# A query product placed between two runs of tiled matmuls in an attention kernel

## The chip, the cores and the metric

The kernel runs on one core of a Trainium2 chip. The metric is the device time of one execution in microseconds (us). Three executions before the change took 798.29, 793.81 and 796.25 us; their median is 796.25 us. A further execution was taken with the hardware profiler: it took 796.67 us, of which the span from the first to the last instruction is 794.9 us. Every time below that belongs to a stage comes from that one execution, counted from the start of the span.

The engines are named as in the profile: PE is TensorE with its matmuls, PEld its weight loads, DVE is VectorE, ACT is ScalarE, POOL is GpSimd, SP is SyncE, which here issues the DMAs.

## The reference

A cross-attention layer with a residual, then a feed-forward layer with low-rank experts and a residual, on 16 batches of 64 tokens of width 512, all in float32. There are 32 heads of width 128. Cut to what matters:

```python
q = (layernorm(x) @ Wq).reshape(b, 64, 32, 128)
k = (ctx @ Wk).reshape(b, 64, 32, 128)
v = (ctx @ Wv).reshape(b, 64, 32, 128)
score = einsum('bqhd,bkhd->bhqk', q, k) / sqrt(128) + position_bias
probs = softmax(where(mask, score, -inf))
x = x + einsum('bhqk,bkhd->bqhd', probs, v).reshape(b, 64, 4096) @ Wo
x = x + base(layernorm(x)) + lora(layernorm(x))   # 8 experts of rank 16
```

## The kernel before

All 1024 tokens are held as 8 tiles of 128. Keys and values of all heads are computed first (lines 312 to 354) and stored to DRAM. Then a loop runs over 16 pairs of heads, numbered p = 0 to 15 (line 504), and the feed-forward layer follows.

Large products are computed to nearly full float32 accuracy from two parts per operand, "high" and "low", in the type float32r: three matmuls stand for one (`mm3`, line 219). Each has a 128x128 weight and 512 moving columns. The projections to keys, values and queries use a Winograd scheme: seven products, in the order 1, 2, 6, 5, 7, 4, 3, in place of eight. For the queries of one pair of heads, each of the seven products is one step of `Queries` (line 454), of six matmuls with 512 columns. A step is called **Q** here. Product 1 fills a PSUM bank, which ACT copies to `u` (line 472); products 6, 7 and 4 go on adding to that bank.

Inside the loop, PE does these jobs for a pair:

- **V** (`pv_mm`, line 429): probabilities of the pair before times its values. The array is cut into four tiles of 64x64. In the trace, each float32 matmul is two weight loads and two matmuls, so that V is 128 weight loads and 128 matmuls of 64 columns.
- **S** (`scores`, line 398): queries times keys, in two tiles of 128x64: 64 weight loads and 64 matmuls of 64 columns. DVE then adds the bias, ACT takes 16 exponentials, and DVE normalises.
- **Q**, seven steps: the queries of the next pair.
- **O** (`proj_o`, line 445), eight steps of six matmuls with 512 columns: the output projection of the pair before.
- **T** (`transpose_p`, line 420), two steps of four transposes: the probabilities of this pair.

The order on PE is the program's own: the whole loop stands under a manual schedule for the tensor engine (line 314). In a pair with p from 1 to 14 it is V, S, and then the string of line 514. The other engines' instructions, SP's DMAs among them, are put in order by a scheduler that sees what each needs. A pair also loads four value blocks (`load_v`, line 375), four key blocks (`load_k`, line 368), two bias blocks (`bias_of`, line 392, with an addition of the mask on POOL), two blocks of the output weight (`load_o`, line 382) and two of query weights (`load_pair`, line 359). The raw query weights of pair p + 2 are loaded, summed on POOL and split by ACT and DVE during pair p.

PSUM has two small banks for S and T, and six banks that Q, O and V take in turn.

Of the kernel before, what the change touches and what calls it, by code (L numbers as in the profile page):

```python
# [23 lines left out]
S = 64  # L24
# [21 lines left out]
def xattn_ffn_kernel(ctx: ExitStack, tc: tile.TileContext, x, ctxT, wq, wk, wv, wo, fside, mask,  # L46
# [17 lines left out]
    def blk(tag, name, dt=F32, shape=(P, 512)):  # L64
        return pools[tag].tile(list(shape), dt, tag=tag, name=name)
# [39 lines left out]
    with ExitStack() as actx:  # L105
# [6 lines left out]
        def small_bank(name):  # L112
            return pss.tile([P, 512], F32, tag="s", name=name)
# [200 lines left out]
        with tc.manual_schedule(engines={nc.tensor.engine}):  # L314
# [44 lines left out]
            def load_pair(p):  # L359
                rq = [blk("raw", "rq", F32, (P, 2, 2, P)) for _ in range(2)]  # L360
                for i in range(2):
                    nc.sync.dma_start(out=rq[i], in_=wq[p, i])
                return rq
# [4 lines left out]
            def load_k(h):  # L368
                kT = []
                for j in range(2):  # L370
                    kT.append(blk("raw", "kT"))
                    nc.sync.dma_start(out=kT[j], in_=kd[h][:, j * HALF:(j + 1) * HALF])
                return kT

            def load_v(p):
                v = []
                for w in range(4):
                    v.append(blk("v", "v", F32, (P, 2, 256)))
                    nc.sync.dma_start(out=v[w], in_=vd[p][:, 2 * w:2 * w + 2, :])
                return v  # L380

            def load_o(p):
                w = []
                for i in range(2):
                    s = blk("raw", "so")
                    nc.sync.dma_start(out=s, in_=wo[p, i])
                    hl = [blk("g", f"w{c}", F32R) for c in "hl"]
                    split(hl[0], hl[1], s)
                    w.append(hl)
                return w  # L390

            def bias_of(h):
                bm = blk("bm", "bm", F32, (P, NT, S))
                nc.sync.dma_start(out=bm, in_=fside[h])
                nc.gpsimd.tensor_tensor(bm, bm, maskb, ALU.add)  # L395
                return bm

            def scores(qT, kT, bm):
                ps = small_bank("pss").rearrange("p (t s) -> p t s", t=NT)
                for t in range(NT):  # L400
                    for a in range(2):
                        n = 4 * (t // 2) + 2 * a + t % 2
                        c = slice((n % 8) * S, (n % 8 + 1) * S)
                        nc.tensor.matmul(ps[a * S:(a + 1) * S, t, :], lhsT=qT[n // 8][:, c],  # L404
                                         rhs=kT[n // 8][:, c], start=True, stop=True)
                p = blk("sn", "p", F32, (P, NT, S))
                nc.vector.scalar_tensor_tensor(p, ps, scale, bm, ALU.mult, ALU.add)
                nm = sm.tile([P, NT], F32, tag="nm", name="nm")
                nc.vector.tensor_reduce(nm, p, AX.X, ALU.max, negate=True)  # L409
                sme = sm.tile([P, NT], F32, tag="sme", name="sme")  # L410
                for t in range(NT):
                    nc.scalar.activation(p[:, t, :], p[:, t, :], AF.Exp, bias=nm[:, t:t + 1],  # L412
                                         accum_out=sme[:, t:t + 1])
                rc = sm.tile([P, NT], F32, tag="rc", name="rc")
                nc.vector.reciprocal(rc, sme)
                nc.vector.tensor_tensor(rc, rc, valid, ALU.mult)
                nc.vector.tensor_tensor(p, p, rc.unsqueeze(2).to_broadcast([P, NT, S]), ALU.mult)  # L417
                return p

            def transpose_p(p):  # L420
                ps = small_bank("pst")
                for g in range(4):
                    nc.tensor.transpose(ps[:, g * P:(g + 1) * P],  # L423
                                        p[:, 2 * g:2 * g + 2, :].rearrange("p t k -> p (t k)"), ident)
                pt = blk("sn", "pt", F32, (P, NT, S))
                nc.scalar.copy(pt, ps.rearrange("p (u q) -> p u q", q=S))
                return pt

            def pv_mm(i, pt, v):
                ps = [bank() for _ in range(2)]  # L430
                for u in range(NT):
                    for b in range(2):
                        r = slice(b * S, (b + 1) * S)
                        for d in range(0, P, S):
                            c = slice(i * P + d, i * P + d + S)
                            nc.tensor.matmul(ps[b][d:d + S, u * S:(u + 1) * S], lhsT=v[u // 2][r, u % 2, c],  # L436
                                             rhs=pt[r, u, :], start=True, stop=True)
                res = []
                for b in range(2):
                    hl = [blk("o", f"o{c}", F32R) for c in "hl"]  # L440
                    split(hl[0], hl[1], ps[b])
                    res.append(hl)
                return res

            def proj_o(t, cts, w):
                ps = bank()
                b, g = divmod(t, 4)
                c = slice(g * P, (g + 1) * P)
                for i, ct in enumerate(cts):
                    mm3(ps, [a[:, c] for a in ct[b]], w[i], i == 0, i == 1)  # L450
                with tc.high_priority(offset=SOON):
                    nc.vector.tensor_tensor(acc[:, t, :], acc[:, t, :], ps, ALU.add)  # L452
# [36 lines left out]
            qs = Queries(load_pair(0), ORDER_Q)  # L489
# [4 lines left out]
            for n, i in enumerate(winograd(mm_tokens(tc_, gv), 2, emit_v(NQ - 1), order=ORDER_Q)):  # L494
                if n == 3:
                    ks = [load_k(0), load_k(1)]
                    bms = [bias_of(0), bias_of(1)]
# [6 lines left out]
            for p in range(NP):  # L504
                last = p + 1 == NP
                if pts is not None:
                    prev = ([pv_mm(i, pts[i], v) for i in range(2)], w)
                ps = [scores(qs.head(i), ks[i], bms[i]) for i in range(2)]
                v = load_v(p)
                if not last:  # L510
                    ks = [load_k(2 * p + 2 + i) for i in range(2)]
                    bms = [bias_of(2 * p + 2 + i) for i in range(2)]
                after = None
                steps = "OOOOOOTOTO" if last else "QQQOOQOQOOQOQOTOT" if p else "QQQQQTQQT"
                pts, t, n = [], 0, 0
                for c in steps:
                    if c == "Q":
                        nxt(1)
                        n += 1
                        if n == 3:  # L520
                            w = load_o(p)
                        if n == 7 and p + 2 < NP:
                            after = Queries(load_pair(p + 2), ORDER)
                        if n == 7 and p + 2 == NP:
                            sar = [blk("raw", "sar", F32, (P, 2, NB)) for _ in range(2)]
                            sbw = [blk("raw", "sbw") for _ in range(KC)]
                            for i in range(2):
                                nc.gpsimd.memset(sar[i][:, :, NAR:NB], 0.0)
                                nc.sync.dma_start(out=sar[i][:, :, 0:NAR], in_=arT[:, 2 * i:2 * i + 2])
                            for kc in range(KC):  # L530
                                nc.sync.dma_start(out=sbw[kc], in_=base_wT[:, kc])
                    elif c == "T":
                        pts.append(transpose_p(ps[len(pts)]))
                    else:
                        proj_o(t, *prev)
                        t += 1
                        if last and t == 2:
                            w = load_o(p)
                qs, nxt = nxt, after
# [168 lines left out]
```

## Time and profile before

| what | value |
|---|---|
| median of three runs | 796.25 us (793.81 to 798.29) |
| the profiled execution: time, span | 796.67 us, 794.9 us |
| granted TensorE clock | 1.00 |
| PE, PEld busy | 775.9 us (98%), 674.7 us (85%) |
| DVE, ACT, POOL busy | 580.0 us (73%), 412.3 us (52%), 143.3 us (18%) |
| DMA queue q1 (data) | 119.42 MB, 45.4% of 16 engines |
| DMA queues q8 and q14 (instructions) | 54 packets, 0.88 MB; 32 packets, 0.26 MB |
| loop over the pairs | from 336.4 us (first S) to 734.1 us (last V) |
| one pair, from V to the next V | 25.58 us in most, up to 27.35 us |
| PE instructions | 6944 weight loads, 6944 matmuls |

A busy share is the union of an engine's instruction times over the span. The ends of matmuls are modelled, so a share near 100% says that PE always had something in flight, and not that it ran at its peak; the step from one start to the next is the better measure of a matmul's cost.

### The profile page before, as it was taken

The page shows a single profiled execution, that of the slowest core. Times are in us where ns is not written, and L with a number is a line of the kernel's source. Part 1 is how long each engine was busy: PE and PEld are TensorE (multiplying, and loading weights), DVE is VectorE, ACT ScalarE, POOL GpSimd, SP SyncE. Part 2 cuts the span into 40 slices and gives each one's busy share as a digit, 9 for nine tenths or more (in the row PEclk, how much of TensorE's full clock was granted, in tenths as well). Part 3 has the DMA queues.
Part 4 walks back from the last instruction along what each step waited for, and adds up shares of the span by engine and source line. Part 5 has one row for each costly group of instructions (what it writes and reads, how often), then busy time and mean ns, then how long its engine had stood idle before and what let it go on. Part 6 is the DMA issues. An engine that isn't in the chain of part 4 may idle for free.

```text
span 794.9 us, 17975 instructions
## 1 busy us (share of the span) xinstructions
PE 775.9 (98%) x6944; PEld 674.7 (85%) x6944; DVE 580.0 (73%) x1056; ACT 412.3 (52%) x1154; POOL 143.3 (18%) x146
## 2 busy tenths in 40 slices
PE   7999999999999999999999999999999999999997
PEld 6989899999999999878888888888888887888786
DVE  6997656565557545687778787788778786878986
ACT  6655444444444445565564556555654555456342
POOL 1021000000006012033211322023211321110352
PEclk9999999999999999999999999999999999999999
DMA  7665545455555443474553454434452455241011
GB/s 262 220 238 199 178 162 179 162 183 174 171 171 175 160 159 133 153 230 149 177 170 89 137 173 161 127 112 161 160 181 79 141 178 168 77 154 54 1 41 66
DMA packets 66374, 120.56 MB, mean 152 GB/s; under 512 B 7536, under 2 KB 8176, under 8 KB 66288
## 3 DMA queue, kind: packets, MB, share of 16 engines
q1 hardware_dynamic: 66288, 119.42, 45.4%
q8 instruction: 54, 0.88, 0.5%
q14 instruction: 32, 0.26, 0.1%
HBM read 83.74 MB, written 35.65 MB: 150 GB/s over the span
## 4 chain that ended last, share of the span: by engine, by line
PE 87%; DVE 7%; ACT 2%; issue 1%; DMA 1%; POOL 0%; ACTq 0%; DVEq 0%; POOLq 0%
PE ps L222 76%; PE pss L404 4%; PE ps L436 4%; PE pst L423 2%; ACT p L412 1%; PE yzv L222 1%; DVE pr L605 1%; DVE x2l L69 1%; DVE o L636 1%; DVE gl L69 1%; DVE nb L94 0%; PE pst L100 0%; DMA raw<-in_wk 0%; DMA vd<-c 0%; ACT lg L594 0%
## 5 line engine op out<-in xcount | busy, mean ns | idle before, releaser
L68 ACT CAST gh<-s 128x512 fp32r<-128x512 f32 (+1 forms) x128 | 65.6, 514 | 144.1 <-PE ps L222 134.0
L69 DVE TENSOR_TENSOR gl<-s,gh 128x512 fp32r<-128x512 f32 (+1 forms) x128 | 72.7, 568 | 44.5 <-ACT gh L68 44.3
L222 PE MATMUL ps<-wh,oh 128*128 128x512 f32 x256 | 101.3, 396 | 0.0
L222 PE MATMUL ps<-wl,oh 128*128 128x512 f32 x256 | 99.8, 390 | 0.0
L222 PE MATMUL ps<-wh,ol 128*128 128x512 f32 x256 | 99.7, 390 | 0.0
L452 DVE TENSOR_TENSOR acc<-acc,ps 128x512 f32<-128x512 f32 x128 | 85.3, 675 | 16.5 <-PE ps L222 15.7
L412 ACT ACTIVATE p<-p,nm 128x64 f32<-128x64 f32 x256 | 85.6, 340 | 6.2 <-DVE nm L409 6.2
L157 POOL TENSOR_TENSOR s<-rq 128x256 f32<-128x256 f32 x32 | 25.1, 784 | 293.4 <-DMA rq<-in_wq 206.0
L395 POOL TENSOR_TENSOR bm<-bm,maskb 128x512 f32<-128x512 f32 x32 | 47.1, 1494 | 74.1 <-DVE maskb L342 40.4
L69 DVE TENSOR_TENSOR gl<-raw,gh 128x512 fp32r<-128x512 f32 x48 | 34.6, 723 | 31.9 <-ACT gh L68 31.9
L222 PEld LDWEIGHTS ps<-wl,oh 128*128 128x128 f32 x256 | 48.0, 188 | 10.1
L222 PEld LDWEIGHTS ps<-wh,ol 128*128 128x128 f32 x256 | 48.1, 188 | 9.8 <-DVE ol L69 0.5
L222 PEld LDWEIGHTS ps<-wh,oh 128*128 128x128 f32 x256 | 48.1, 188 | 9.5
L68 ACT CAST gh<-raw 128x512 fp32r<-128x512 f32 x48 | 29.7, 621 | 48.2 <-PE ps L222 36.5
L69 DVE TENSOR_TENSOR ol<-ps,oh 128x512 fp32r<-128x512 f32 x64 | 39.8, 683 | 15.6 <-ACT oh L68 15.6
L412 ACT ACTIVATION_READ_ACCUMULATOR p<-p,nm 128x1 f32 x256 | 49.1, 192 | 0.0
L479 DVE TENSOR_TENSOR q<-u,ps 128x512 f32<-128x512 f32 x48 | 32.7, 681 | 12.6 <-PE ps L222 12.3
L417 DVE TENSOR_TENSOR p<-p,rc 128x512 f32<-128x512 f32 x32 | 39.5, 1234 | 1.1
L68 ACT CAST wh<-so 128x512 fp32r<-128x512 f32 x32 | 19.7, 616 | 37.7 <-PE ps L222 37.1
L404 PE MATMUL pss<-kT,q 128*64 128x64 f32 x1024 | 34.9, 224 | 4.5 <-issue 4.5
L68 ACT CAST oh<-ps 128x512 fp32r<-128x512 f32 x64 | 33.1, 591 | 7.7 <-PE ps L436 7.7
L404 PEld LDWEIGHTS pss<-kT,q 128*64 128x64 f32 x1024 | 31.9, 138 | 5.9 <-issue 4.5
(226 smaller groups left out, 2246.7 us busy)
## 6 DMA issues: line engine op xcount, KB each, us to landing
kd<-c SPq DMA_DIRECT2D x64, 256.0 KB, 2.9
vd<-c SPq DMA_DIRECT2D x64, 256.0 KB, 2.7
v<-vd SPq DMA_DIRECT2D x64, 256.0 KB, 4.6
kT<-kd SPq DMA_DIRECT2D x64, 256.0 KB, 5.3
raw<-in_wk SPq DMA_DIRECT2D x32, 256.0 KB, 3.2
raw<-in_wv SPq DMA_DIRECT2D x32, 256.0 KB, 3.2
bm<-in_fside SPq DMA_DIRECT2D x32, 256.0 KB, 6.0
rq<-in_wq SPq DMA_DIRECT2D x32, 256.0 KB, 5.2
```

What stands on the lines that cost most here:

```text
L68: nc.scalar.copy(hi, src)
L69: (lo_eng or nc.vector).tensor_tensor(lo, src, hi.bitcast(F32), ALU.subtract)
L157: self.eng.tensor_tensor(r, a, b, op)
L222: nc.tensor.matmul(o, lhsT=a, rhs=b, start=first and n == 0, stop=last and n == 2, skip_group_check=True)
L395: nc.gpsimd.tensor_tensor(bm, bm, maskb, ALU.add)
L404: nc.tensor.matmul(ps[a * S:(a + 1) * S, t, :], lhsT=qT[n // 8][:, c], rhs=kT[n // 8][:, c], start=True, stop=True)
L412: nc.scalar.activation(p[:, t, :], p[:, t, :], AF.Exp, bias=nm[:, t:t + 1], accum_out=sme[:, t:t + 1])
L417: nc.vector.tensor_tensor(p, p, rc.unsqueeze(2).to_broadcast([P, NT, S]), ALU.mult)
L423: nc.tensor.transpose(ps[:, g * P:(g + 1) * P], p[:, 2 * g:2 * g + 2, :].rearrange("p t k -> p (t k)"), ident)
L436: nc.tensor.matmul(ps[b][d:d + S, u * S:(u + 1) * S], lhsT=v[u // 2][r, u % 2, c], rhs=pt[r, u, :], start=True, stop=True)
L452: nc.vector.tensor_tensor(acc[:, t, :], acc[:, t, :], ps, ALU.add)
L479: nc.vector.tensor_tensor(self.blocks[key], s[u], b[bk], ALU.add)
```

## The change

In pairs 1 to 14 the first Q step of the pair is put between V and S; the remaining steps keep their places. In pair 0 and in the last pair S still comes first. Nothing is computed more or less. As the score code moves into the loop over the step string, the loads of the values now stand ahead of the scores in the program, and the loads of keys and bias stand directly behind the scores.

```diff
-                ps = [scores(qs.head(i), ks[i], bms[i]) for i in range(2)]
                 v = load_v(p)
-                if not last:
-                    ks = [load_k(2 * p + 2 + i) for i in range(2)]
-                    bms = [bias_of(2 * p + 2 + i) for i in range(2)]
                 after = None
-                steps = "OOOOOOTOTO" if last else "QQQOOQOQOOQOQOTOT" if p else "QQQQQTQQT"
+                steps = "SOOOOOOTOTO" if last else "QSQQOOQOQOOQOQOTOT" if p else "SQQQQQTQQT"
                 pts, t, n = [], 0, 0
                 for c in steps:
-                    if c == "Q":
+                    if c == "S":
+                        ps = [scores(qs.head(i), ks[i], bms[i]) for i in range(2)]
+                        if not last:
+                            ks = [load_k(2 * p + 2 + i) for i in range(2)]
+                            bms = [bias_of(2 * p + 2 + i) for i in range(2)]
+                    elif c == "Q":
                         nxt(1)
                         n += 1
```

In the built program PE's order differs only in that place, 14 times. On SP, the order of a pair's loads becomes: four value blocks, two of query weights, bias, keys, bias, keys, keys, keys; before, it was three value blocks, two of query weights, the fourth value block, two of bias, four of keys. On ACT, the second copy to `u` (product 6) stands behind eight exponentials rather than six. On DVE, the first split of an output weight block stands ahead of the two score additions rather than behind them, and the first two additions of O to the accumulator stand behind the normalisation of the first head rather than around it.

## The prediction

> **What bounds the kernel.** I read the shares and the chain of waits first, then the waits of PE, then the starts of PE's instructions in single pairs. From the page, the shares, the instruction queue and the chain:
>
> ```profile
> PE 775.9 (98%) x6944; PEld 674.7 (85%) x6944; DVE 580.0 (73%) x1056; ACT 412.3 (52%) x1154; POOL 143.3 (18%) x146
> ...
> q8 instruction: 54, 0.88, 0.5%
> ...
> PE 87%; DVE 7%; ACT 2%; issue 1%; DMA 1%; POOL 0%; ACTq 0%; DVEq 0%; POOLq 0%
> ```
>
> PE carries 87% of the chain, so a microsecond on PE in the loop is one at the end. What PE waits for, from the view of waits (total, times, longest):
>
> ```profile
> PE ps L222 <- ACT t1h L68: 5.3, 1, 5.3
> PE pss L404 <- issue: 4.5, 6, 1.4
> PE ps L635 <- DVE hl L69: 1.2, 3, 0.9
> ```
>
> The first is at the start, the third in the feed-forward layer. The second is all that the loop loses, it is in S alone, and "issue" says that no semaphore was waited for. The timeline of PE in pair 2 and in pair 3 (start, length, operation, count):
>
> ```profile
> 376.70 0.60 PE L423 MATMUL pst<-ident,p 128*128 128x128 f32 x4
> 377.23 2.10 PE L436 MATMUL ps<-pt,v 64*64 64x64 f32 x128
> 379.25 1.03 PE L404 MATMUL pss<-kT,q 128*64 128x64 f32 x28
> 381.33 1.28 PE L404 MATMUL pss<-kT,q 128*64 128x64 f32 x36 [1.05 <-issue]
> 382.54 0.50 PE L222 MATMUL ps<-t1h,gh 128*128 128x512 f32 x1
> ```
>
> ```profile
> 403.57 0.60 PE L423 MATMUL pst<-ident,p 128*128 128x128 f32 x4
> 404.10 2.10 PE L436 MATMUL ps<-pt,v 64*64 64x64 f32 x128
> 406.13 2.09 PE L404 MATMUL pss<-kT,q 128*64 128x64 f32 x64
> 408.14 0.50 PE L222 MATMUL ps<-t1h,gh 128*128 128x512 f32 x1
> 408.48 0.40 PE L222 MATMUL ps<-t1h,gl 128*128 128x512 f32 x1
> 408.71 0.40 PE L222 MATMUL ps<-t1l,gh 128*128 128x512 f32 x1
> ```
>
> In pair 3, S takes 408.14 - 406.13 = 2.01 us; in pair 2 it breaks off after 28 matmuls and takes 382.54 - 379.25 = 3.29 us. Measured like this, S is longer by 0.78, 1.28, 0.77, 0.83, 0.58 and 1.77 us in pairs 1, 2, 5, 9, 12 and 13, and never in the other eight of the fourteen that change: **6.01 us in all**.
>
> **What the stalls are.** Counting PE's instructions in the trace from its first, weight loads and semaphore waits included, the six that come late have the numbers 4801, 5313, 7105, 9409, 11201 and 11713: each is 193 above a multiple of 256. Queue q8 moves 54 packets of 16 KB, one for each 258 of PE's 13,954 instructions. So PE's program comes in blocks of 256 instructions, and PE stood at the edge of a block not yet there. The packets' records agree: one starts at 352.92, 378.92, 457.08, 559.93, 637.63 and 664.12 us, and PE goes on 2.62, 2.41, 2.40, 2.39, 2.60 and 2.41 us later. In the six cases these packets start 0.8 to 1.6 us after PE has begun a block. V is 256 instructions in 2.03 us and S is 128 in 2.01 us, while six Q matmuls are 12 in 1.36 us; only V with S behind it can use up 256 instructions in less time than a refill takes. It happens where a block begins some 30 to 130 instructions into V, as the next then begins in S. That holds for the six pairs and for pair 6, where the block came just in time (packet at 481.74, used at 484.15 us, no gap).
>
> Here a rule speaks against the change's worth. The Trainium skill, page "Runtime: NRT & Kernel Launch", section "Instruction fetch mechanics", says that instructions come in 16 KiB blocks of 256, that PE holds 2048 of them and that crossing a block is mostly hidden. The block size agrees with the trace; the hiding does not, at six edges of 54. By the rule nothing is to be saved and only the cost below remains; by the rows up to 6.01 us are. I take the rows.
>
> **What the change removes.** The same instructions stand before V, and the number of instructions of a pair stays, so blocks begin at the same places of V. The edge in S is now reached later: six Q matmuls add 1.59 us (below), and as they are 12 instructions the edge lies 12 of S's 128 sooner, 0.19 us; the refill gains 1.40 us. Five of the six stalls are shorter and go to nothing; pair 13 keeps 1.77 - 1.40 = 0.37 us. **Saved: 6.01 - 0.37 = 5.64 us.** If packets start as late or later in other executions, up to the 6.01 us are there to lose or to win; the lower end is nothing.
>
> **What it adds.** PE's array is 64x64 tiles in V, 128x64 in S, whole in Q, O and T. Before, a pair has three switches (T to V, V to S, S to Q); after, four (T to V, V to Q, Q to S, S to Q). The Trainium skill, page "TensorEngine Tiling (Array Packing)", section "Tiling Modes", says that a change of tiling mode drains TensorE; it has no price. The trace does, in pair 3: from the last start of one kind to the first of the next it is 0.148 us for V to S, 0.151 for S to Q and 0.202 for T to V, where the step within the kind is 0.058, 0.058 and 0.108: about 0.093 us is added at each, whatever the kinds. Then the first weights load in the open: the first Q matmul takes 0.335 us to the next start in place of 0.227, and some steps after it 0.2345.
>
> A switch from Q to S is not in the trace. Lower end: it drains behind other work, and only the 0.108 us of the first Q matmul are paid again: 14 x 0.108 = 1.5 us. Upper end: S waits for the modelled end of the last Q matmul (0.39 us after its start) and 0.093 us more: 0.26 + 0.108 + 0.03 = 0.40 a pair, 5.6 us. Nearest is T to V, which also goes from the whole array to tiles: the step plus 0.093. So the moved Q takes 0.335 + 4 x 0.2345 + 0.227 + 0.093 = 1.59 us where six steps of 0.227 are 1.36: 0.23 us a pair. V to Q replaces V to S at the same 0.15, and the Q step behind S pays what the first paid before. **Added: 14 x 0.234 = 3.3 us.**
>
> **What moves beside it.**
> - S starts 1.59 us later, so its key buffers come free later and key loads are issued later, by as much. Keys of the next pair landed by 423.4 us in pair 3 and are used at 431.7: hidden.
> - SP's queue is in order. The query-weight loads still wait for S's first half and now for the first split of an output weight, which comes earlier since Q does; the bias loads wait for the score additions, about 1.5 us later. POOL ends its bias additions at 419.6 us in pair 3; they are needed at 433.
> - The first Q needs the bank of the seventh O, whose addition on DVE ended at 428.2 us before a V at 429.7: free. Product 6 adds to the bank that ACT copies after product 1; with S between, this copy has 2 us more.
> - The copy of product 6 waits behind eight exponentials. By an estimate from the rows of pair 3 (S half done at 408.7, 0.7 us each for the score addition and the maximum) the exponentials start near 410.3 us, as before (410.6), because the cast and the copy ahead of them come before S's end; product 7, which needs the copy, starts at 417.8. The normalised second head is ready at 420.1 us and transposed at 429.2. Cost: nothing; if the cover went, 7 us would have to go first.
>
> **Sum** against the profiled execution (796.67 us: span 794.9 and 1.8 around it): -5.64 + 3.28 = -2.4 us, 794.3 us. That execution lies 0.4 us above the median of the three, so from 796.25 I forecast **793.9 us**.
>
> **The rivals.**
> - **Larger gain.** The drain after Q hides (1.5 us) and all 6.01 us go: -4.5, 791.7 us. For it: pair 13's rest depends on one packet that started 1.6 us after its block began, which another execution need not repeat. Against it: every switch in the trace pays 0.09 us.
> - **The toll stands alone, slower.** Executions without the profiler have no refill stalls, or new ones replace them; PE pays the fourth switch: 796.25 + 3.3 = 799.5 us, at the upper toll 801.9. It decides as soon as the stalls saved are below 3.3 us. For it: that I see refills only in the profiled execution, and the rule above. Against it: that execution is as long as the others.
> - **A new wait.** The later S makes its pair's chain (score additions, exponentials, transposes) end too late, or the changed order on SP delays a load for Q: 1 us a pair would be +14 us and 808 us with the rest. Against it: the margins above, 7 us and more.
> - **It does nothing it says.** Excluded: the built order has the six matmuls between V and S 14 times.
>
> **Numbers.** 0.5% is 4 us and about what a measurement can tell from no change: faster means below 792.3, slower above 800.2. Forecast 0.50, almost all of it "within"; larger gain 0.30, of which 0.25 past the line; toll alone 0.14, of which 0.06 past it; a new wait 0.06, nearly all past it. With 0.05 of the forecast's own spread on the fast side: faster 0.30, same 0.59, slower 0.11. The forecast's own range is 792 to 796; to leave out 2 in 10 it has to reach into the larger gain and the toll: 790.3 to 798.6.
>
> **What would show it.** S at 2.01 us in pairs 1, 2, 5, 9 and 12 and at most 0.4 us more in 13; the wait of PE for "issue" in S below 1 us; moved Q to S 0.32 us from last start to first; undisturbed pairs 0.23 us longer than 25.58. I am wrong if S still breaks off in most of the six, if undisturbed pairs grow by over 0.4 us, or if PE waits for DVE, ACT or a DMA in the loop.

## The result, and the profile after

Over 20 executions each, the median went from 797.64 us to **794.34 us** (793.03 to 796.92). The ratio on record is 0.997, 95% interval 0.996 to 0.9979, or 2.4 us (1.7 to 3.2). It is an estimate of its own and not the quotient of these two medians, which differ by 3.3 us; against 44 other executions of the kernel before (median 796.8 us) the difference is 2.5 us. The gain is real and small, between 2 and 3 us.

From the page of the kernel after: the shares, the instruction queue and the chain.

```profile
PE 778.5 (98%) x6944; PEld 673.7 (85%) x6944; DVE 589.1 (74%) x1056; ACT 413.0 (52%) x1154; POOL 144.0 (18%) x146
...
q8 instruction: 54, 0.88, 0.5%
...
PE 88%; DVE 7%; ACT 2%; DMA 2%; issue 1%; POOL 0%; SPq 0%; ACTq 0%; DVEq 0%; POOLq 0%
```

PE is busy for 2.6 us *more* than before, and the kernel is faster. A share of busy time can't tell a stall that went from a drain that came: the ends of the last matmuls before a switch are counted as busy. The number of refill packets is the same; what changed is whether PE waits for them. The waits of PE (total, times, longest):

```profile
PE ps L222 <- ACT t1h L68: 5.4, 2, 4.7
PE ps L636 <- DVE hl L69: 1.2, 3, 0.9
PE ps L222 <- ACT u L193: 1.1, 1, 1.1
PE ps L222 <- DVE q L479: 0.8, 1, 0.8
```

The row "pss L404 <- issue: 4.5, 6, 1.4" of before has no counterpart. Pair 2, which had lost 1.28 us in S, in the timeline of PE (start, length, operation, count):

```profile
378.51 2.10 PE L436 MATMUL ps<-pt,v 64*64 64x64 f32 x128
380.54 0.50 PE L222 MATMUL ps<-t1h,gh 128*128 128x512 f32 x1
380.87 0.40 PE L222 MATMUL ps<-t1h,gl 128*128 128x512 f32 x1
381.11 0.40 PE L222 MATMUL ps<-t1l,gh 128*128 128x512 f32 x1
381.34 0.40 PE L222 MATMUL ps<-t1h,gh 128*128 128x512 f32 x1
381.57 0.39 PE L222 MATMUL ps<-t1h,gl 128*128 128x512 f32 x1
381.80 0.40 PE L222 MATMUL ps<-t1l,gh 128*128 128x512 f32 x1
382.13 2.08 PE L404 MATMUL pss<-kT,q 128*64 128x64 f32 x64
384.14 0.50 PE L222 MATMUL ps<-t2h,gh 128*128 128x512 f32 x1
```

Six query matmuls stand between 380.54 and 382.13, and S then runs through its 64 matmuls in 384.14 - 382.13 = 2.01 us. The refill packet of this edge starts at 380.12 us, and the instruction at the edge (number 5313, the same as before) runs at 382.76. Before, the packet started at 378.92 and PE arrived first. Both packets start about equally long after PE has begun a block (1.19 us after, 1.27 before); what changed is how soon the next edge comes. The moved step has given the packet its time.

Of the fourteen pairs that changed, only pair 13 still breaks off in S:

```profile
665.75 0.40 PE L222 MATMUL ps<-t1l,gh 128*128 128x512 f32 x1
666.07 2.32 PE L404 MATMUL pss<-kT,q 128*64 128x64 f32 x64
668.32 0.50 PE L222 MATMUL ps<-t2h,gh 128*128 128x512 f32 x1
```

Here S takes 668.32 - 666.07 = 2.25 us, some 0.23 over. All stalls in S together are 0.24 us, where they were 6.01. And every pair pays: one without a stall lasts 25.81 us from V to V, where it was 25.58.

| part of the profiled execution | before | after |
|---|---|---|
| time | 796.67 us | 795.94 us |
| first S of pair 0 starts at | 336.44 us | 338.00 us |
| pair 0, first S to V of pair 1 | 14.43 us | 14.68 us |
| pairs 1 to 14, from V to V | 364.24 us | 361.63 us |
| stalls in S | 6.01 us | 0.24 us |
| undisturbed pair | 25.58 us | 25.81 us |

The two profiled executions differ by only 0.7 us. The pairs gained 2.6 us, pair 0 lost 0.25 (its wait for DVE's q, line 479, was 0.60 us and is 0.84), and this execution had lost 1.6 us ahead of the loop, where nothing was edited and PE, POOL and SP do the same work in the same order. Over the eight profiled executions of this study, the first S starts anywhere from 335.19 to 338.00 us, and the difference is there within the first 85 us. The three latest (337.50 to 338.00) belong to the three kernels that have the moved step in pair 1; with one execution each, that may be chance. The timed differences follow the loops: a loss of 1.6 us in every execution would leave 0.7 us of gain, and the interval begins at 1.7. So below, stages of single executions are compared only inside the loop, from the start of the first S of pair 0 to the start of the last V ("the loop": 395.59 us before, 393.28 after), and whole times only as medians.

### The profile page after: what moved, and what is told of

The parts are those of the page before. It is cut to its first block, busy times and chain, and to the rows that moved or that the text cites. A ratio compares the mean times of both kernels' runs of the same rounds, so it can differ in the third digit from the quotient of the medians.

```text
span 794.2 us, 18002 instructions
## 1 busy us (share of the span) xinstructions
PE 778.5 (98%) x6944; PEld 673.7 (85%) x6944; DVE 589.1 (74%) x1056; ACT 413.0 (52%) x1154; POOL 144.0 (18%) x146
## 4 chain that ended last, share of the span: by engine, by line
PE 88%; DVE 7%; ACT 2%; DMA 2%; issue 1%; POOL 0%; SPq 0%; ACTq 0%; DVEq 0%; POOLq 0%
PE ps L222 77%; PE pss L404 4%; PE ps L436 4%; PE pst L423 2%; PE yzv L222 1%; ACT p L412 1%; DMA cT<-in_ctxT 1%; DVE o L637 1%; DVE pr L606 1%; DVE x2l L69 1%; DVE nb L94 1%; DVE gl L69 0%; PE pst L100 0%; DVE we L608 0%; DMA so<-in_wo 0%
## 5 line engine op out<-in xcount | busy, mean ns | idle before, releaser
L395 POOL TENSOR_TENSOR bm<-bm,maskb 128x512 f32<-128x512 f32 x32 | 50.0, 1582 | 73.1 <-DVE maskb L342 40.8
L69 DVE TENSOR_TENSOR gl<-rq,gh 128x256 fp32r<-128x256 f32 x48 | 32.9, 687 | 11.4 <-ACT gh L68 11.4
L479 DVE TENSOR_TENSOR q<-u,ps 128x512 f32<-128x512 f32 x48 | 32.6, 680 | 10.6 <-PE ps L222 10.6
L92 POOL TENSOR_TENSOR rs<-rs,nhalf 128x1 f32<-128x1 f32 x16 | 9.5, 595 | 152.1 <-DVE rs L91 109.2
L404 PEld LDWEIGHTS pss<-kT,q 128*64 128x64 f32 x1024 | 31.2, 138 | 5.6 <-PE ps L222 5.0
L436 PEld LDWEIGHTS ps<-pt,v 64*64 64x64 f32 x2048 | 31.4, 135 | 3.3 <-ACT gh L68 2.2
```

The source lines that it names most:

```text
L69: (lo_eng or nc.vector).tensor_tensor(lo, src, hi.bitcast(F32), ALU.subtract)
L92: nc.gpsimd.tensor_tensor(rs, rs, nhalf[:, 0:n], ALU.pow)
L479: nc.vector.tensor_tensor(self.blocks[key], s[u], b[bk], ALU.add)
```

## The experiments

The theory says that two independent terms make the result: stalls at the edges of PE's instruction blocks, which depend only on where an edge falls, and a toll of 0.23 us for each pair with the fourth switch, which is paid everywhere. The main rival says that the order does it: V and S back to back wait for something of their own, or Q in front is better by itself. Four kernels ran beside 44 executions of the kernel before (median 796.8 us), two more beside 9 (796.77 us). Each ratio is to these and, as above, is not exactly the quotient of the medians.

### Query product first in the six stalled pairs only

```diff
-steps = ... else "QSQQOOQOQOOQOQOTOT" if p else "SQQQQQTQQT"
+steps = ... else "QSQQOOQOQOOQOQOTOT" if p in (1, 2, 5, 9, 12, 13) else "SQQQOOQOQOOQOQOTOT" if p else "SQQQQQTQQT"
```

> The query step stands between V and S only in pairs 1, 2, 5, 9, 12 and 13, those whose S broke off before the change; the other eight have V directly before S. My theory (S breaks off where a block of PE's instructions is not yet there, at places fixed by the count of instructions): S takes 2.0 us in all fourteen pairs, at most 0.3 us more in 13; six pairs grow by 0.23 us. Saved 5.8, paid 1.4: 4.4 us below the kernel before, ratio 0.9945. Rival 1 (the stall is a property of V directly before S, and only turned up in these six by chance): about as much stall as before turns up in the eight unprotected pairs, ratio 0.998 to 1.002. Rival 2 (the gain of the change is made by the new order on ACT, DVE and SP, in every pair alike): 6/14 of the 3.3 us measured, ratio 0.998.

Measured, over 11 executions: 793.73 us, ratio 0.996 (0.9947 to 0.9973). The stalls in S are 0.10 us (pair 2) and 0.20 us (pair 13), 0.30 in all; the six pairs last 25.81 us and their stall, the eight others 25.58 (pair 8 with 0.15 more in V). The loop is 3.91 us shorter than before, with 0.28 us lost in pair 0. Saved stalls (6.01 - 0.30) less six tolls (6 x 0.23) are 4.3 us. Direction and place are as expected; the time is just short of the forecast, whose ratio lies below the interval. That the gain over the changed kernel is real isn't shown by the medians alone (the intervals of 0.996 and 0.997 overlap); the pairs of the profile show it.

### Query product first in the eight other pairs only

The same edit with the two strings exchanged.

> The query step stands between V and S only in the other eight pairs (3, 4, 6, 7, 8, 10, 11, 14). My theory: S breaks off in pairs 1, 2, 5, 9, 12 and 13 as before, by 6 us in all, and the eight pairs pay 0.23 us each: 1.9 us above the kernel before, ratio 1.0024. Rival 1 (stall by chance): the stalls are in other pairs of those unprotected or fewer, ratio below 1. Rival 2 (the order on the other engines gains): 8/14 of the 3.3 us, ratio 0.9976.

Measured, over 22 executions: 797.99 us, ratio 1.0014 (1.0006 to 1.0023): slower. Its waits of PE hold the old row:

```profile
PE pss L404 <- issue: 4.1, 6, 1.2
```

The stalls stand in the same six pairs, with 0.50, 1.28, 0.77, 1.02, 0.53 and 1.50 us, 5.60 in all, and the eight reordered pairs last 25.81 us. So the same edit costs time where no edge lies in S. An order that were better by itself would have won here. The size is somewhat less than expected, as in the run before: the loop is 1.35 us longer, of which 8 x 0.23 = 1.9 is toll and -0.4 are stalls that happened to be shorter.

### The order of before, shifted by 128 instructions

No-operations on PE carry its count of instructions forward and leave the order of the work alone. Spread over the steps of pair 0:

```diff
+FILL = {0: 128}
...
-                for c in steps:
+                for m, c in enumerate(steps):
+                    k, s = FILL.get(p, 0), len(steps) - 3
+                    for _ in range(k * (m - 2) // s - k * (m - 3) // s if m > 2 else 0):
+                        nc.tensor.nop("fill", nofuse=True)
```

> The kernel before with 128 no-operations in PE's steps of pair 0, so that every later block of 256 instructions begins 128 instructions sooner in its pair. My theory: S breaks off in pairs 3, 4, 7, 10, 11 and 14 in place of 1, 2, 5, 9, 12 and 13, 4 to 8 us in all; ratio 0.997 to 1.003. Rival (data, DMAs or the place in the loop): S breaks off in 1, 2, 5, 9, 12 and 13 as before.

Measured, over 16 executions: 798.31 us, ratio 1.0024 (1.0012 to 1.0035). The stalls moved to the pairs named beforehand. Where the block begins, counted in PE's instructions from the start of V, and the stall of S in us:

```
pair                1    2    3    4    5    6    7    8    9   10   11   12   13   14   15
block, before     130   58  -13  172  101   30  215  144   73    2  187  116   45  230  159
stall, before     .78 1.28    -    -  .77    -    -    -  .83    -    -  .58 1.77    -    -
block, shifted      2  -70  115   44  -27  -98   87   16  -55  130   59  -12  -83  102   31
stall, shifted      -    -  .85 1.57    -    -  .94  .24    -  .47 1.28    -    -  .77  .39
```

Pair 3, whose S ran unbroken before, in this kernel's timeline of PE (its line numbers are one higher):

```profile
405.31 1.85 PE L405 MATMUL pss<-kT,q 128*64 128x64 f32 x56
407.80 0.45 PE L405 MATMUL pss<-kT,q 128*64 128x64 f32 x8 [0.63 <-issue]
408.18 0.50 PE L223 MATMUL ps<-t1h,gh 128*128 128x512 f32 x1
```

S breaks off after 56 of 64 matmuls. Data, tiles and order of that pair are those of before; only the edge has come to lie in it. PE's count at the late instruction is again 193 above a multiple of 256. Three stalls were not expected by name: 0.24 us in pair 8, 0.39 us in pair 15, and 1.78 us in pair 1, between V and S, at the first instruction of S (4801, also 193 above a multiple). In pair 1 the block begins 2 instructions into V, as in pair 10 before, which had no stall; but there the packet for the next block started 2.26 us before the block began, and here 1.52 us after. The no-operations just ahead had probably used up PE's lead; the run after the next puts them elsewhere for that reason. With 6.51 us of stalls in S, these 1.78 and 0.44 more in pair 0, where the 128 no-operations stand, the loop is 2.64 us longer than before.

### The order of before, with the edges steered clear

A pair has 583 instructions, so an edge moves by 583 - 2 x 256 = 71 from pair to pair. Five groups of no-operations, 276 in all, keep it out of S:

```diff
-FILL = {0: 128}
+FILL = {0: 104, 3: 43, 6: 43, 9: 43, 12: 43}
```

> The kernel before, with its order V, S, Q, and 276 no-operations spread over PE's Q and O steps of pairs 0, 3, 6, 9 and 12, so that no block of 256 instructions begins between 28 and 138 instructions into a V. My theory: no S breaks off and there is no fourth switch: 6.0 us below the kernel before, ratio 0.9925, and 2.7 us below the changed kernel, if no-operations hide beside the matmuls; if each costs PE 50 ns in the open, 14 us are lost and the ratio is 1.010. Rival (the stalls have to do with the data, the DMAs or the place in the loop, not with the count of instructions): S breaks off in pairs 1, 2, 5, 9, 12 and 13 as before, ratio 1.000.

Measured, over 6 executions: 791.1 us, ratio 0.9933 (0.9916 to 0.9949). The shares and the instruction queue on its page:

```profile
PE 773.9 (98%) x6944; PEld 673.7 (85%) x6944; DVE 579.8 (74%) x1056; ACT 412.4 (52%) x1154; POOL 144.7 (18%) x146
...
q8 instruction: 55, 0.90, 0.5%
```

One packet more, and PE busy for less: the kernel has 276 more instructions and ends 5.7 us earlier by the medians. One stall is left, 0.64 us in pair 1, whose block begins at instruction 26 of V, at the rim of the stalling region:

```profile
PE pss L405 <- issue: 0.4, 1, 0.4
```

Pairs 4, 7, 10 and 13, whose blocks begin at 25, have none. Every later pair lasts 25.58 us (one 25.59), those with 43 no-operations too. So these cost nothing that can be seen; they stand among the steps of 512 columns, each of which keeps PE for 0.23 us. With the order untouched, a gain of the same kind and about twice the size appears: what the moved step gains comes from the edges, and not from the order as such.

### The same, with the first group ahead of the loop

The 104 no-operations of pair 0 stand in the last values product instead (14 or 15 behind each Winograd step), so that pair 1 doesn't have them just ahead of it.

```diff
+                for _ in range(15 if n else 14):
+                    nc.tensor.nop("fill", nofuse=True)
...
-FILL = {0: 104, 3: 43, 6: 43, 9: 43, 12: 43}
+FILL = {3: 43, 6: 43, 9: 43, 12: 43}
```

> The kernel before, filled as the run with 276 no-operations, but the 104 that stood in pair 0 now stand in the last product of the values, ahead of the loop, where PE uses few instructions per microsecond. My theory: the 0.65 us by which S of pair 1 still broke off go as well; no S breaks off; 6.0 us below the kernel before, ratio 0.9925. Rival (the rest in pair 1 is not a matter of how fast the block ahead was used up): 0.65 us stay, ratio 0.9933.

Measured, over 5 executions: **790.3 us**, ratio **0.9923** (0.9906 to 0.9939): faster than both kernels. Pair 2 in its timeline of PE:

```profile
374.40 2.10 PE L437 MATMUL ps<-pt,v 64*64 64x64 f32 x128
376.42 2.09 PE L405 MATMUL pss<-kT,q 128*64 128x64 f32 x64
378.44 0.50 PE L223 MATMUL ps<-t1h,gh 128*128 128x512 f32 x1
```

V and S stand back to back as before, and S takes 2.02 us; there is no drain for a fourth switch. The only stall is 0.28 us in pair 4. The loop is 6.52 us shorter than before; 5.7 of that are stalls, and 0.80 is pair 0, which takes 13.63 us in place of 14.43: it no longer shows the wait for DVE's q (L479). Why pair 0 gained was not followed up. Between this run and the one before it, 0.82 of the 1.05 us by which the loops differ are pair 0; the intervals of the two ratios overlap.

In pair 1 the block still begins 26 instructions into V, and its stall of 0.64 us is gone. The packet for the next block started 0.30 us after that block began in the run before, and here 0.68 us before it. So it is not the place of the edge alone that counts, but also when the packet starts, and the no-operations just ahead had made it later.

### The changed order, with the same filling

The changed kernel with the two additions of the run before. Both kernels have their edges out of S, so what differs is the toll and whatever else the order does.

> The changed kernel with the same fill: no block can be late in either, so against the run above only the fourth switch is left. My theory: each of pairs 1 to 14 takes 0.23 us more than 25.58, 3.3 us above the run above; ratio to the kernel before 0.9966. Rival (the step between V and S does something else that is good, on ACT, DVE or SP): below 0.996. Rival (the switch is cheaper outside the profiled execution, as the runs of six and of eight pairs leave open): 1.5 us, ratio 0.9944.

Measured, over 5 executions: 793.46 us, ratio 0.9957 (0.9943 to 0.9971), 3.2 us above the run before. In this profile there is no stall in S at all, and pairs 1 to 14 last 25.81 us each (pair 1 25.83). Pair 2, in its timeline of PE:

```profile
377.07 2.10 PE L437 MATMUL ps<-pt,v 64*64 64x64 f32 x128
379.10 0.50 PE L223 MATMUL ps<-t1h,gh 128*128 128x512 f32 x1
...
380.36 0.40 PE L223 MATMUL ps<-t1l,gh 128*128 128x512 f32 x1
380.69 2.09 PE L405 MATMUL pss<-kT,q 128*64 128x64 f32 x64
382.70 0.50 PE L223 MATMUL ps<-t2h,gh 128*128 128x512 f32 x1
```

The loop is 3.04 us longer than in the run before, or 3.3 when that one's remaining stall is taken off. The ratio alone excludes neither rival: 0.9957 lies below 0.996, and the interval takes in 0.9944. What decides is the profile, in which each of the fourteen pairs is longer by 0.23 us. **The toll is 14 x 0.23 = 3.2 us**, now measured without the stalls.

## Why the prediction was right, point by point

- **What bounds the kernel**: right for pairs 1 to 14. The reading that the stalls in S are "all that the loop loses" passed over three waits at its two ends: 0.56 and 0.60 us in pair 0, for ACT and DVE, and 0.43 us in pair 15. The forecast put pair 0 at nothing; it cost 0.25 us.
- **What the stalls are**: right, and shown. Edges moved by 128 instructions move the stalls to the predicted pairs; edges out of S remove them. The rule that crossings are mostly hidden (the Trainium skill, "Runtime: NRT & Kernel Launch", "Instruction fetch mechanics") gave 0 to save. By count it holds, since 48 of 54 edges are hidden; by time it doesn't, since the others cost 6 us, and the ratios of the two kernels filled in the old order are worth 5.3 and 6.1 us (0.8 of the latter in pair 0). Of the 2048 instructions that PE is said to hold nothing shows. In all eight traces the packets of q8 are as many as the edges (54 or 55). The n-th packet starts between 4.6 us before and 6.5 us after PE passes the n-th edge, and PE never passes the next edge less than 2.17 us after that packet's start. So the refill runs one block ahead, and PE stalls when it comes to the next edge before some 2.4 us have passed since that start.
- **What the change removes**: predicted 5.64 us, measured 6.01 - 0.24 = 5.77. The delay of the edge by 1.40 us was enough in five pairs; pair 13 kept 0.23 us where 0.37 were forecast. There the packet started later than before (1.80 us after its block began, where it was 1.62), but PE went on 2.17 us after it, not 2.41.
- **What it adds**: the moved Q takes 380.54 to 382.13 = 1.59 us, as predicted, and its last start to the first S 0.33 us (predicted 0.32). The unseen switch was priced between 1.5 and 5.6 us; the value taken from its nearest row, T to V, 3.3 us, is what the last experiment measures. The view of the line of S shows the idle time of the engine before it, weight loads and matmuls together, before and after:

```profile
its engine sat idle before it (us, times) until:
  issue: 9.0, 11
  DMA acc<-in_x: 0.3, 1
```

```profile
its engine sat idle before it (us, times) until:
  PE ps L222: 5.0, 14
  issue: 0.5, 2
```

  S's weight loads wait in fourteen pairs for the end of the last Q matmul (0.36 us each), where before it was "issue" that ended most of it. Most of the 0.36 us lies beside Q's own last matmul; only 0.093 us and Q's first weights make the pair longer.
- **What moves beside it**: free, as argued. In pair 3 the exponentials start at 410.72 us (estimate 410.3, before 410.61), the normalised second head is ready at 419.2 (forecast 420.1), and POOL ends its bias additions at 420.40 (before 419.6). PE waits for no other engine in S.
- **Sum**: predicted -2.4 us; the pairs 1 to 14 show -2.6 us, the loop -2.3 and the timed ratio -2.4 (the medians -3.3). The parts agree one by one, so the sum is no accident; that it agrees to 0.1 us is in part luck, as the interval is 1.5 us wide.
- **The rivals**: *larger gain* would have needed a drain that hides, and all fourteen pairs pay 0.23 us. *The toll alone* was a real danger: it is what the run on the eight other pairs does, and it would have decided had the stalls been under 3.3 us. The record gives a span and a granted clock for every timed execution, so it doesn't show how an execution without any profiling behaves. *A new wait*: none in pairs 1 to 14. In pair 15, V waits 0.26 us for the probabilities (ACT's `pt`, line 426), a row that the view of before lacks; V lasts 2.52 us there, where it was 2.24.

What stays open: between executions a stall varies (pair 9 had 0.83 us before and 1.02 in the run on eight pairs, pair 1 had 0.78 and 0.50), which may be why these two partial runs moved the time a little less than expected. Why a packet starts up to 1.6 us after a block begins in one V and ahead of it in another, and whether other DMA traffic delays it, was not tried.

## What to carry to other kernels

A wait that the profile calls "issue", in the middle of an unbroken run of short instructions and at numbers that agree modulo 256, was here a late instruction refill, and not a property of the work around it: count the instructions and look at the instruction queue's packets before reordering. Moving work between two dense runs can cover such a wait, but it charges its own price in every pair, here 3.2 of the 5.8 us saved. Shifting the edges with no-operations among long matmuls removed nearly all of the stalls at no cost that could be seen in pairs 1 to 14; it has to be fitted anew whenever the number of instructions changes, and can make things worse when it is off, as the shift by 128 did.

## What the runs showed of the hardware

- 43 no-operations on PE in a pair, among steps of 512 columns, left it at 25.58 us. With 128 in pair 0, that pair took 14.87 us in place of 14.43, and the edge behind it came 1.78 us late (pair 1 of the shifted kernel).
- The six stalled instructions come 2.39 to 2.62 us after the start of their packets, and no instruction at an edge in the eight traces comes less than 2.17 us after its packet. A block that begins 30 to 130 instructions into V was followed by a stall in 13 of 14 pairs (the orders of before and of the shifted kernel); at 25 and 26 in two of ten (0.28 us and 0.64 us, in the two filled kernels of the old order).
- A switch of tiling cost about 0.09 us each, and a run of whole-array matmuls behind a tiled one takes another 0.11 us for its first matmul (0.335 us to the next start in place of 0.227): together, and with slightly longer steps, 0.23 us for a piece of work moved in between two tiled runs.
- Ahead of the loop, single executions of the eight kernels, whose work there is the same, differ by up to 2.8 us in the profile (335.19 to 338.00 us to the first S), which is more than this change brings.
